# Turning a group's probabilities in two parts, and issuing the grams' rows from GpSimd

## The chip, the cores and the metric

The kernel runs on one core of a Trainium2 chip. Five engines of that core run their own streams of instructions and wait for each other by semaphores: TensorE (PE) multiplies matrices, VectorE (DVE), ScalarE (ACT) and GpSimd (POOL) work on elements, SyncE (SP) only issues DMA transfers. The metric is the device time of one execution in microseconds. The kernel before takes 424.8 us, the median of three runs (424.51 to 426.21).

## The reference

Cross attention with 20 heads of 16 channels over 8 batches: 112 queries, 375 context rows of 512 channels, of which the last four are image prompts.

```python
q = heads(hidden_states @ W_q)
k_t, v_t = heads(text_ehs @ W_k), heads(text_ehs @ W_v)
probs_t = softmax(einsum('bhsd,bhtd->bhst', q, k_t) * attn_scale)
text_out = einsum('bhst,bhtd->bhsd', probs_t, v_t)
attn_scores = einsum('bhsd,bhnd->bhsn', q, k_ip) * attn_scale
qsem = _l2norm(einsum('bhst,bte->bhse', probs_t, text_ehs))
sem = einsum('bhse,bne->bhsn', qsem, _l2norm(ip_ehs))
probs_ip = softmax(attn_scores + SEM_SCALE * sem) * spatial_mask[None, None, :, None]
out = (text_out + einsum('bhsn,bhnd->bhsd', probs_ip, v_ip)) @ W_out + b_out + hidden_states
```

All arithmetic is float32.

## The kernel before, in words

The norm of `qsem` is taken without forming `qsem`: it is p G p with G the gram matrix of the batch's context, so for every head the probabilities are multiplied once by a matrix `u` that holds the upper half of G (with doubled off-diagonal parts), the four prompts' products, a column of ones and the head's value columns.

The work goes in 40 steps `(b, g)`: 8 batches of 5 groups of 4 heads. In the main loop (35 steps) a step does this:

- `scores` (L709) multiplies one head's queries by its keys into a PSUM bank of a ring of two (`ps_sc`). `probabilities` (L738) takes the row maximum on VectorE (L742), the exponential on ScalarE (L745), and copies the prompts' four columns out (L747); `sent` (L751) has SyncE issue the transfer of the head's probabilities into `xg` (L754), one of two buffers, where they stand in blocks of 32 rows. This is done two steps ahead of the step that multiplies them: heads 2 and 3 at the head of the step (`now`), heads 0 and 1 during it (`then`). In the last steps of batch 6 `ahead` (L1238) draws some heads further forward; those in `more` are held, that is, sent later than computed.
- `transposed` (L756) turns the group of the next step: one VectorE transposition of all 12 blocks of `xg` into `xgT` (L762, 128 x 1536), for the last batch two of six blocks.
- `multiplied` (L768) is the main product: for each of 12 blocks j it issues four matmuls, one for each head, in four row groups of TensorE, into four PSUM banks (L781). Block j needs columns 32j to 392, so blocks get narrower: 392, 360, 328, ... 40. The right side is `u`; from batch 1 on, blocks 0 to 3 read its first third (c = 0), 4 to 7 the second, 8 to 11 the last. The function is a generator, and other work is issued between its blocks.
- After the product ScalarE copies the last 21 columns of each bank (`value_sums`, L794) and VectorE reduces the rest against the probabilities (`reduced`, L827, four instructions). Only then are the banks free for the next step, which uses the same four.
- `placed` (L681, L688) has GpSimd copy the next group's value columns into `u`, one copy for each third. The copy of a third must follow the blocks of this step that read that third, and precede those of the next step.
- `between` (L1116) gives TensorE the next batch's projections: the gram at g = 0 (`gram`, L516), values at g = 1, keys and values at 2, keys at 3, and the end of the batch before.

The next batch's gram is doubled by ScalarE into `ug` (L507), masked by GpSimd (L508, three instructions), and then carried by 16 transfers of 99 KB, `gram_to_groups` (L549, L553), into the other of two buffers `u`: four blocks of rows, each to four heads. In the kernel before, SyncE issues them in portions of two or four over steps g = 1 to 3, between the transfers of probabilities, context and values; batch 0's last block is issued by ScalarE.

The order of TensorE, SyncE, VectorE and ScalarE is that of the program text in the main loop. GpSimd's order there is made by a scheduler; only in the last batch it is that of the text too. A DMA waits on the issuing engine's stream for one of eight completion semaphores, so the ninth issue waits until the first transfer has landed.

Of the kernel before, what the change touches and what calls it, by code (L numbers as in the profile page):

```python
# [20 lines left out]
def kernel(  # L21
# [14 lines left out]
    nc = tc.nc  # L36
    P = 128
    B, S, C = x.shape
# [507 lines left out]
            doubled(ps[c][:, : T - c * P], c, half[:, c])  # L546
            yield

    def gram_to_groups(b, blocks, eng=nc.sync, parts=range(GROUP)):  # L549

        for q in blocks:
            for a in parts:
                eng.dma_start(  # L553
                    st[b]["u"][a * RG : (a + 1) * RG, q * GW : (q + 1) * GW],
                    ug[q * RG : (q + 1) * RG, :],
                )
# [152 lines left out]
    def scores(b, g, a, early=False, ps=None):  # L709
        s = st[b]  # L710
        _, qm, j = queries[b]
        i, r = g // 2, g % 2
        if early and (g + a // 2) % 2:

            ps = ps_qd.tile([P, 512], F32, tag="qd", name=f"ps_s_{b}_{g}_{a}")
        elif ps is None:
            ps = ps_sc.tile([P, 512], F32, tag="sc", name=f"ps_s_{b}_{g}_{a}")
        w = T if b > 0 else TT
        nc.tensor.matmul(  # L719
            ps[:S, :w],  # L720
            qm[a * RG : (a + 1) * RG, i, r, j * S : (j + 1) * S],
            s["kT"][a * RG : (a + 1) * RG, i, :w],
            start=True,
            stop=True,
        )
        s["sc", g, a] = ps
# [11 lines left out]
    def probabilities(b, g, a, hold=False):  # L738
        s = st[b]
        ps = s.pop(("sc", g, a))  # L740
        nmx = small.tile([S, 1], F32, tag="nmx", name=f"nmx_{b}_{g}_{a}", bufs=4)
        nc.vector.tensor_reduce(nmx, ps[:S, :TT], AX.X, ALU.max, negate=True)  # L742
        if ("p", g) not in s:
            s["p", g] = home(b, g)
        nc.scalar.activation(s["p", g][:, a, :], ps[:S, :TT], AF.Exp, bias=nmx)  # L745
        if b > 0:
            nc.scalar.copy(s["ipl"][:, groups[g][a], :], ps[:S, TT:T])  # L747
        if not hold:
            sent(b, g, a)

    def sent(b, g, a):  # L751

        xg = x_ring[(b * NG + g) % NX]
        nc.sync.dma_start(xg[a * RG : a * RG + S // QN, :, :TT], st[b]["p", g][:, a, :])  # L754

    def transposed(b, g):  # L756

        xg = x_ring[(b * NG + g) % NX]
        xT = work.tile([P, BLK, P], F32, tag="xgT", name=f"xgT_{b}_{g}")
        n = BLK // 2 if b == B - 1 else BLK  # L760
        for j in range(0, BLK, n):
            nc.vector.transpose(  # L762
                xT[:, j : j + n].rearrange("p j (k q) -> p q j k", q=QN),
                xg[:, :, j * RG : (j + n) * RG].rearrange("p q (j k) -> p q j k", k=RG),
            )
        st[b]["xT", g] = xT

    def multiplied(b, g):  # L768
        s = st[b]
# [406 lines left out]
    order_values()  # L1176
    drain(products)
    nc.scalar.preload_act_table(AF.Exp)
    gram_to_groups(0, range(QN - 1))
    run(("v", 0), lambda: values(0))  # L1180
    run(("q", 0), lambda: project_queries(pairs[0]), 3)
    gram_to_groups(0, (QN - 1,), nc.scalar)
# [22 lines left out]
    load_embed(nc.sync, wkip_sb, w_k_ip)  # L1205
    load_embed(nc.sync, wvip_sb, w_v_ip)
    placed(0, 0)
    transposed(0, 0)
    run(("k", 0), None)
    run(("v", 1), lambda: values(1))  # L1210
    more_constants()
# [38 lines left out]
    for n, (b, g) in enumerate(steps[:-NG]):  # L1250
        now, more, then = ahead(n)
        late = (b, g) == (0, NG - 2)
        for c, a in now if not late else ():
            scores(*c, a)
            probabilities(*c, a)
        for j, _ in enumerate(multiplied(b, g)):
            if j == 0:
                for c, a in now if late else ():
                    scores(*c, a)
                    probabilities(*c, a)  # L1260
                for c, a in more:
                    scores(*c, a, ps=bank(f"ps_s_{c[0]}_{c[1]}_{a}"))
                    probabilities(*c, a, hold=True)
            if j == 6:
                for c, a in then:
                    scores(*c, a)
            if j == 2:
                if g == 0:
                    gram_banks(b + 1)
                transposed(*steps[n + 1])  # L1270
                for c, a in more:
                    sent(*c, a)
                if 1 <= g <= 3:
                    gram_to_groups(b + 1, {1: (0,), 2: (1,), 3: (3,)}[g], parts=halves[g == 2])
                for c, i in x_loads.get((b, g), ())[: int(n > 0)]:
                    load_x_blocks(c, i)

                if g in (1, 2) and b > 0:
                    run(("f", b - 1), None)
        value_sums(b, g)  # L1280
        if g == 2 and b > 0:
            run(("f", b - 1), None)
        if n == NG - 1:
            run(("t", b), lambda: prompt_logits(b))
        for c, a in then:
            probabilities(*c, a)
        if n == len(steps) - NG - 1:
            sums = shared(b, g, GROUP // 2)
            next(sums)
            reduced(b, g, 2)  # L1290
        else:
            reduced(b, g)
        placed(*steps[n + 1])
        if g == 0 and b > 1:
            run(("f", b - 2), None)
        load_rest(n)
        if n == 0:
            load_next(2)
        if g in ctx_blocks and b < B - 3:
            load_ctx_blocks(b + 3, ctx_blocks[g])  # L1300
        for c, i in x_loads.get((b, g), ())[1:]:
            load_x_blocks(c, i)
        if g == 1:
            gram_to_groups(b + 1, (0,), parts=halves[1])
            gram_to_groups(b + 1, (1,), parts=halves[0])
        elif g == 2:
            gram_to_groups(b + 1, (2,))
        elif g == 3:
            gram_to_groups(b + 1, (3,), parts=halves[1])
            values_to_groups(b + 1)  # L1310
        if g in (2, 3) and b == 0:
            run(("pp",), None)
        if (b, g) == (B - 2, 0):
            prompt_values_by_head()
        if (b, g) == (B - 2, 1):
            bd = load_prompt_values_by_head()
        if (b, g) == (B - 2, 3):
            own_channels(bd)
        if g == 0 and b > 0:
            prompt_values(b - 1)  # L1320
        between(b, g)
        if g == 1:
            values_to_dram(b + 1, nc.sync, 0, 2)
        if g == 2:
            values_to_dram(b + 1, nc.sync, 2)
# [17 lines left out]
    for g in range(NG):  # L1343
        if g == 1:
            keys3 = last_keys(b, bank(f"ps_k_{b}_{FULL}", spare=True))
            next(keys3)
            next(keys3)
            run(("q", b), None)
            nc.scalar.preload_act_table(AF.Sqrt)
            run(before, None, 3)  # L1350
        for j, _ in enumerate(multiplied(b, g)):
            if g == 0 and j in (0, 3):
                for a in (2, 3) if j == 0 else (0, 1):
                    coming(NG - 2, a, bank(f"ps_s_{b}_{NG - 2}_{a}", spare=a > 1))
            if g == 0 and j in (2, 3):
                if j == 2:
                    transposed(b, 1)
                for a in (2, 3) if j == 2 else (0, 1):
                    sent(b, NG - 2, a)
            if g == 1 and j in (2, 3):  # L1360
                for a in ((3, 2), (1, 0))[j - 2]:
                    ps = ps_qd.tile([P, 512], F32, tag="qd", name=f"ps_s_{b}_{NG - 1}_{a}")
                    coming(NG - 1, a, ps)
            if g == 1 and j == 4:
                run(before, None)
            if g == 3 and j == 8:
                drain(sums)
            if 0 < g < NG - 1 and j in (QN - 1, 2 * QN - 1):
                placed(b, g + 1, (j // QN,))
        if g == NG - 1:  # L1370
            break
        n = (3, 3, 2, 1)[g]
        ahead, sums = sums, shared(b, g, n)
        next(sums)
        reduced(b, g, n)
        if g < NG - 2:
            value_sums(b, g, n)
            transposed(b, g + 2)
            placed(b, g + 1, range(NT) if g == 0 else (NT - 1,))
            next(sums)  # L1380
            drain(ahead)
        if g == 0:
            run(before, lambda: finish(b - 1, bd=bd[:, 0]))
            with_bias(b)
            run(("f", b - 2), None)
        if g == 2:
            nc.scalar.preload_act_table(AF.Sqrt)
        if g == 3:
            value_sums(b, g, 1, 3)
            placed(b, g + 1, (NT - 1,))  # L1390
            drain(sums)
            value_sums(b, g, 3)
            first = finish(b, (0, FULL * HC), bd=bd[:, 1])
            for _ in range(4):
                next(first)
# [70 lines left out]
```

## Time and profile before

| what | value |
|---|---|
| median of three runs | 424.8 us |
| profiled execution | 424.01 us, span 422.3 us |
| TensorE busy | 413.7 us (98%) |
| VectorE busy | 332.3 us (79%) |
| ScalarE busy | 185.2 us (44%) |
| GpSimd busy | 111.6 us (26%) |
| issues of `u<-ug` | 124 by SyncE, 4 by ScalarE |
| issues of `xg<-p` | 156 by SyncE |

Shares of busy time are over the whole span. Issuing a DMA is not counted as busy; it stands in the timeline with the engine's name and a q (SPq). The idle time of an engine stands in brackets behind the instruction that ended it, with what released it.

### The profile page before, as it was taken

What the parts mean: (1) busy time and instruction counts of PE and PEld (TensorE: products, weight loads), DVE (VectorE), ACT (ScalarE), POOL (GpSimd) and SP (SyncE); (2) the same over time, 40 slices, a digit from 0 to 9 for tenths busy, and PEclk for the clock granted to TensorE, in tenths of its full rate; (3) what the DMA queues carried; (4) which work ended last, traced back from release to release, by engine and by line L of the source; (5) the groups of instructions that cost most, each with busy time, mean ns of one, the idle gap of its engine ahead of it and who ended that gap; (6) DMA issues with size and microseconds to landing.
All of it is one profiled execution on the core that took longest, in us unless ns stands there. A gap on an engine that the chain in (4) does not pass through costs nothing.

```text
span 422.3 us, 14016 instructions
## 1 busy us (share of the span) xinstructions
PE 413.7 (98%) x5496; PEld 324.4 (77%) x5496; DVE 332.3 (79%) x693; ACT 185.2 (44%) x647; POOL 111.6 (26%) x277
## 2 busy tenths in 40 slices
PE   8999999999998999999999999999999999989996
PEld 8867768888776877788778877778778887778983
DVE  5036788879896978898789987887898987978774
ACT  2344332337333363344434363333634463445784
POOL 6411110012060111511142220602124222505540
PEclk9999999999999999999999999999999999999999
DMA  8676856666765555675656555655655456466200
GB/s 240 203 191 192 190 144 182 164 170 153 193 167 147 159 167 160 161 177 158 164 151 165 136 167 157 167 146 152 169 153 153 125 165 179 121 168 167 80 2 29
DMA packets 61687, 65.84 MB, mean 156 GB/s; under 512 B 22072, under 2 KB 55648, under 8 KB 61622
## 3 DMA queue, kind: packets, MB, share of 16 engines
q1 hardware_dynamic: 60990, 63.98, 56.6%
q8 instruction: 44, 0.72, 0.8%
q10 hardware_dynamic: 632, 0.96, 0.7%
q14 instruction: 21, 0.17, 0.1%
HBM read 20.23 MB, written 5.32 MB: 61 GB/s over the span
## 4 chain that ended last, share of the span: by engine, by line
PE 91%; DMA 2%; DVE 2%; issue 2%; ACT 2%; SPq 1%; POOL 0%; DVEq 0%; POOLq 0%
PE ps_qd L781 39%; PE ps_v L611 14%; PE ps_k L577 11%; PE ps_s L719 9%; PE ps_g L535 7%; PE ps_q L377 3%; PE ps_o L995 2%; PE ps_g L491 1%; DMA xg<-p 1%; DMA vipd<-ipkv 1%; DVE nmx L742 1%; PE ps_w L467 1%; PE ps_o L950 1%; PE ps_c L450 1%; DVE xgT L762 1%
## 5 line engine op out<-in xcount | busy, mean ns | idle before, releaser
L781 PE MATMUL ps_qd<-u,xgT 32*112 32x360 f32 (+11 forms) x3840 | 218.4, 351 | 2.0 <-POOL u L688 2.0
L781 PEld LDWEIGHTS ps_qd<-u,xgT 32*112 32x112 f32 x3840 | 187.3, 172 | 28.5 <-POOL u L688 3.1
L762 DVE STREAM_TRANSPOSE xgT<-xg 128x1536 f32<-128x1536 f32 (+1 forms) x45 | 119.7, 2677 | 11.4 <-DMA xg<-p 5.6
L745 ACT ACTIVATE p<-ps_s,nmx 112x371 f32<-112x371 f32 x156 | 85.2, 588 | 58.4 <-DVE nmx L742 46.5
L742 DVE TENSOR_REDUCE nmx<-ps_s 112x1 f32<-112x371 f32 x160 | 76.8, 524 | 28.2 <-PE ps_s L719 27.4
L827 DVE CUSTOM_DVE_ANT_0 junk<-ps_qd,p 112x371 f32<-112x371 f32 x146 | 79.1, 542 | 17.4 <-PE ps_qd L781 1.4
L688 POOL COPY u<-vr 128x64 f32<-128x64 f32 x120 | 26.0, 239 | 152.4 <-PE ps_qd L781 91.8
L719 PE MATMUL ps_s<-kT,qm 32*112 32x375 f32 (+1 forms) x320 | 65.7, 496 | 0.0
L611 PE MATMUL ps_v<-wv_sb,ctxT 128*128 128x384 f32 (+1 forms) x192 | 63.0, 477 | 0.0
L611 PEld LDWEIGHTS ps_v<-wv_sb,ctxT 128*128 128x128 f32 x192 | 35.7, 190 | 20.9
L794 ACT COPY pvs<-ps_qd 112x21 f32<-112x21 f32 x151 | 16.3, 189 | 75.1 <-PE ps_qd L781 72.3
L577 PE MATMUL ps_k<-ctxT,wk_sb 128*128 128x371 f32 x136 | 46.9, 488 | 0.2 <-DVE ctxT L458 0.2
L577 PEld LDWEIGHTS ps_k<-ctxT,wk_sb 128*128 128x128 f32 x136 | 24.4, 189 | 14.0 <-issue 0.5
L719 PEld LDWEIGHTS ps_s<-kT,qm 32*112 32x112 f32 x320 | 23.3, 170 | 12.3 <-issue 10.8
L535 PE MATMUL ps_g<-ctxT 128*32 128x375 f32 (+11 forms) x672 | 30.4, 333 | 0.0
L535 PEld LDWEIGHTS ps_g<-ctxT 128*32 128x32 f32 x672 | 27.7, 110 | 2.0
L618 ACT COPY vext<-ps_v 128x384 f32<-128x384 f32 (+1 forms) x24 | 11.2, 466 | 39.5 <-PE ps_v L611 39.0
L747 ACT COPY ipl<-ps_s 112x4 f32<-112x4 f32 x140 | 24.5, 175 | 0.0
L386 DVE TENSOR_SCALAR qm<-ps_q,emask 128x224 f32<-128x224 f32 (+1 forms) x25 | 9.0, 395 | 18.3 <-PE ps_q L377 18.2
L970 POOL TENSOR_TENSOR wv<-vip,w 112x1280 f32<-112x1280 f32 x6 | 14.8, 2466 | 26.2 <-DVE w L910 26.2
L437 DVE STREAM_TRANSPOSE ctxT<-ct 128x512 f32<-128x512 f32 x18 | 19.9, 1107 | 0.0
L508 POOL TENSOR_TENSOR ug<-ug,half 128x128 f32<-128x128 f32 (+1 forms) x24 | 10.5, 449 | 30.9 <-ACT ug L507 30.9
(174 smaller groups left out, 319.3 us busy)
## 6 DMA issues: line engine op xcount, KB each, us to landing
xg<-p SPq DMA_DIRECT2D x156, 162.3 KB
u<-ug SPq DMA_DIRECT2D x124, 99.0 KB
ct<-in_ctx_dram SPq DMA_DIRECT2D x24, 176.0 KB
vr<-vd SPq DMA_DIRECT2D x32, 120.0 KB
vip<-vipd SPq DMA_DIRECT2D x6, 560.0 KB
vd<-vext SPq DMA_DIRECT2D x7, 320.0 KB
vd<-vext SPq DMA_DIRECT2D x7, 160.0 KB
out_dram<-ob SPq DMA_DIRECT2D x8, 140.0 KB
```

The lines of the kernel that those rows point to most:

```text
L437: nc.vector.transpose(ctxT[:, :, c * P : (c + 1) * P].rearrange("p e (j i) -> p j e i", i=RG), ct[:, some, :].rearrange("p j (k e) -> p j ...
L535: nc.tensor.matmul(ps[c][q * RG : (q + 1) * RG, j * RG - c * P : T - c * P], ctxT[:, e, j * RG : (j + 1) * RG], ctxT[:, e, j * RG : T], st ...
L577: nc.tensor.matmul(ps[:, :TT], wk_sb[:, e, i * P : (i + 1) * P], s["ctxT"][:, e, :TT], start=(e == 0), stop=(e == NE - 1),)
L611: nc.tensor.matmul(ps[:, :w], ctxT[:, e, c * P : (c + 1) * P], wv_sb[:, e, :w], start=(e == 0), stop=(e == NE - 1),)
L688: nc.gpsimd.tensor_copy(v, dealt(b, c, s["vr"][:, c * QN : (c + 1) * QN, g, :]))
L719: nc.tensor.matmul(ps[:S, :w], qm[a * RG : (a + 1) * RG, i, r, j * S : (j + 1) * S], s["kT"][a * RG : (a + 1) * RG, i, :w], start=True, st ...
L742: nc.vector.tensor_reduce(nmx, ps[:S, :TT], AX.X, ALU.max, negate=True)
L745: nc.scalar.activation(s["p", g][:, a, :], ps[:S, :TT], AF.Exp, bias=nmx)
L747: nc.scalar.copy(s["ipl"][:, groups[g][a], :], ps[:S, TT:T])
L762: nc.vector.transpose(xT[:, j : j + n].rearrange("p j (k q) -> p q j k", q=QN), xg[:, :, j * RG : (j + n) * RG].rearrange("p q (j k) -> p ...
L781: nc.tensor.matmul(banks[a][:S, j * RG : UW], xT[a * RG : (a + 1) * RG, j, :S], region(b, c)[a * RG : (a + 1) * RG, q, j * RG - c * P :], ...
L827: nc.vector.tensor_tensor_reduce(out=junk, in0=ps[:S, :TT], in1=s["p", g][:, a, :], scale=1.0, scalar=0.0, op0=ALU.mult, op1=ALU.add, accu ...
```

## The change

Two things change. The turn of a group in the main loop becomes a generator: eight blocks are turned at j = 2, then, at j = 5 instead of 6, the scores of heads 0 and 1 are issued, followed at once by their maxima and exponentials (they stood after `value_sums` before), and then the other four blocks are turned. Heads whose buffer is the one just turned are sent after that. The last batch's own turns keep their two halves. The main loop so has 34 more transpositions, and each is 1024 or 512 wide instead of 1536.

And `gram_to_groups` issues from GpSimd unless told otherwise; only three blocks of batch 0 stay with SyncE and one with ScalarE. That moves 112 issues, 16 for each of seven batches.

```diff
-    def gram_to_groups(b, blocks, eng=nc.sync, parts=range(GROUP)):
+    def gram_to_groups(b, blocks, eng=nc.gpsimd, parts=range(GROUP)):
...
-    def transposed(b, g):
+    def turned(b, g, n=BLK // 2):
         xg = x_ring[(b * NG + g) % NX]
         xT = work.tile([P, BLK, P], F32, tag="xgT", name=f"xgT_{b}_{g}")
-        n = BLK // 2 if b == B - 1 else BLK
-        for j in range(0, BLK, n):
+        st[b]["xT", g] = xT
+        for j0 in range(0, BLK, n):
+            j1 = min(j0 + n, BLK)
             nc.vector.transpose(
...
-        st[b]["xT", g] = xT
+            yield
...
-    gram_to_groups(0, range(QN - 1))
+    gram_to_groups(0, range(QN - 1), nc.sync)
...
-            if j == 6:
+            if j == 5:
                 for c, a in then:
                     scores(*c, a)
+                held = more + [(c, a) for c, a in then if c == steps[n + LEAD + 1]]
+                for c, a in then:
+                    probabilities(*c, a, hold=(c, a) in held)
+                drain(turn)
+                for c, a in held:
+                    sent(*c, a)
             if j == 2:
                 if g == 0:
                     gram_banks(b + 1)
-                transposed(*steps[n + 1])
-                for c, a in more:
-                    sent(*c, a)
+                turn = turned(*steps[n + 1], 2 * QN)
+                next(turn)
...
-        for c, a in then:
-            probabilities(*c, a)
```

In the built program GpSimd's stream for one batch (here the part after batch 3's masks of the next gram; the batches 1 to 6 are alike) stands in this order, L553 being the moved issues, L877 the division that stood at L876, and L688 one third of `placed`:

```
L508 TensorTensor ug<-ug,half x3
L553 DMACopy u<-ug 32x792 x3
L877 TensorTensor attn<-pvs,zr 112x320
L553 DMACopy u<-ug 32x792 x5
L688 TensorCopy u<-vr 128x4x16
L553 DMACopy u<-ug 32x792 x6
L688 TensorCopy u<-vr 128x4x16
L553 DMACopy u<-ug 32x792 x2
L688 TensorCopy u<-vr 128x4x16
```

The three L688 there are `placed(b, 2)`, thirds 0, 1 and 2. In the kernel before the same stream is L508 x3, L876, L688 x3. In batch 0 the order after the masks is 11 issues, third 0 of `placed(0, 2)`, 5 issues, thirds 1 and 2.

More of the change, by code (lines that the diff above doesn't have):

```diff
@@ L754, in sent @@
         nc.sync.dma_start(xg[a * RG : a * RG + S // QN, :, :TT], st[b]["p", g][:, a, :])
-    def transposed(b, g):
+    def turned(b, g, n=BLK // 2):
         xg = x_ring[(b * NG + g) % NX]
         xT = work.tile([P, BLK, P], F32, tag="xgT", name=f"xgT_{b}_{g}")
-        n = BLK // 2 if b == B - 1 else BLK
-        for j in range(0, BLK, n):
+        st[b]["xT", g] = xT
+        for j0 in range(0, BLK, n):
+            j1 = min(j0 + n, BLK)
             nc.vector.transpose(
-                xT[:, j : j + n].rearrange("p j (k q) -> p q j k", q=QN),
-                xg[:, :, j * RG : (j + n) * RG].rearrange("p q (j k) -> p q j k", k=RG),
+                xT[:, j0:j1].rearrange("p j (k q) -> p q j k", q=QN),
+                xg[:, :, j0 * RG : j1 * RG].rearrange("p q (j k) -> p q j k", k=RG),
             )
-        st[b]["xT", g] = xT
+            yield
     def multiplied(b, g):
@@ L1207 @@
     placed(0, 0)
-    transposed(0, 0)
+    drain(turned(0, 0, BLK))
     run(("k", 0), None)
@@ L1356 @@
                 if j == 2:
-                    transposed(b, 1)
+                    drain(turned(b, 1))
                 for a in (2, 3) if j == 2 else (0, 1):
@@ L1377 @@
             value_sums(b, g, n)
-            transposed(b, g + 2)
+            drain(turned(b, g + 2))
             placed(b, g + 1, range(NT) if g == 0 else (NT - 1,))
```

## The prediction

> **What bounds the kernel now.** I read the page's busy times and chain first, then the busy times by stretch, then TensorE's timeline for its pauses.
>
> ```profile
> span 422.3 us, 14016 instructions
> PE 413.7 (98%) x5496; PEld 324.4 (77%) x5496; DVE 332.3 (79%) x693; ACT 185.2 (44%) x647; POOL 111.6 (26%) x277
> ...
> PE 91%; DMA 2%; DVE 2%; issue 2%; ACT 2%; SPq 1%; POOL 0%; DVEq 0%; POOLq 0%
> ```
>
> ```profile
> 280.00:340.00 60.00, 60.00 (x879) 48.06 (x875) 51.34 (x109) 26.27 (x100) 14.31 (x34) 1.00 0.54 146
> 340.00:400.00 60.00, 58.58 (x819) 47.38 (x815) 49.26 (x99) 32.73 (x116) 23.55 (x40) 1.00 0.55 152
> ```
>
> ```profile
> 87.65 3.89 PE L781 MATMUL ps_qd<-u,xgT 32*112 32x392 f32 x54 [0.62 <-POOL u L688]
> ...
> 135.91 0.54 PE L568 MATMUL ps_k<-ident,k 128*128 128x128 f32 x3 [1.32 <-ACT ipl L747]
> ...
> 379.99 1.29 PE L781 MATMUL ps_qd<-u,xgT 32*112 32x392 f32 x10 [1.36 <-POOL u L688]
> ```
>
> TensorE is the bound: from 280 to 340 us it is busy 60.00 us of 60, in the next stretch, with the last pause, 58.58, both at a granted clock of 1.00 (the columns are length, then busy time of PE, PEld, DVE, ACT and POOL, then clock). Where it never pauses nothing can be gained; only its three pauses above, 0.62 + 1.32 + 1.36 = 3.30 us, can go. But anything that comes late for a product is paid in full.
>
> **What the change takes away.** The pauses go back to SyncE.
>
> ```profile
> 80.32 1.23 SPq L553 DMA_DIRECT2D u<-ug  x2
> 81.60 2.17 SPq L636 DMA_DIRECT2D vr<-vd  x4
> 87.36 0.59 POOL L688 COPY u<-vr 128x64 f32<-128x64 f32 x3 [6.55 <-DMA vipd<-ipkv]
> ...
> 128.75 2.02 SPq L553 DMA_DIRECT2D u<-ug  x2
> 131.90 2.97 DVE L762 STREAM_TRANSPOSE xgT<-xg 128x1536 f32<-128x1536 f32 x1 [2.62 <-issue]
> ...
> 372.90 2.14 SPq L553 DMA_DIRECT2D u<-ug  x2
> 375.09 2.15 SPq L636 DMA_DIRECT2D vr<-vd  x4
> 379.70 0.59 POOL L688 COPY u<-vr 128x64 f32<-128x64 f32 x3 [10.89 <-DMA xg<-p]
> ```
>
> ```profile
> L553 SPq DMA_DIRECT2D u<-ug x124: 575/589/2139, 14.9 to 374.3; - x124
> ```
>
> The first and the last pause are value rows that land late, issued behind gram rows; in the second a group turned 2.62 us late made the exponentials late that free a bank. Without 112 issues of 0.589 us, 16 for a batch, SyncE reaches each of these transfers at least two issues (1.2 us) sooner, and the probabilities of heads 0 and 1 are sent sooner too, since their exponentials no longer stand behind `value_sums`. I take all of 3.30 us as gone; left is what is late next, at worst none of it goes.
>
> **The turn in two parts.** VectorE's price is the fixed part of one more transposition.
>
> ```profile
> L762 DVE STREAM_TRANSPOSE xgT<-xg 128x1536 f32<-128x1536 f32 x35 | 104.6, 2989 | 11.4 <-DMA xg<-p 5.6 <-issue 3.0 <-DMA ct<-in_ctx_dram 2.6
> ...
> L437 DVE STREAM_TRANSPOSE ctxT<-ct 128x512 f32<-128x512 f32 x18 | 19.9, 1107 | 0.0
> ```
>
> From 512 to 1536 columns is 1882 ns, 1.84 ns each; so 1024 cost 2.05 us, and the two parts 3.16 us against 2.99, 0.17 us more in each of 34 steps. It matters where VectorE is last at the banks:
>
> ```profile
> 225.98 0.54 DVE L827 CUSTOM_DVE_ANT_0 junk<-ps_qd,p 112x371 f32<-112x371 f32 x1
> 226.47 3.41 PE L781 MATMUL ps_qd<-u,xgT 32*112 32x392 f32 x48
> ```
>
> There, from group 3 to 4, the fourth bank is free at 226.52 and wanted at 226.47: no slack. VectorE runs without a break from the step before, so up to two of these 0.17 us show, 0.3 us in each of six batches: 0 to 2.1 us. If TensorE pauses in a batch for something longer (next part), VectorE catches up meanwhile and the price is nothing; I take that. The maxima only change places with the last third of the turn, and nothing waits longer for either: the next step's product wants `xgT` only after `between`. If a maximum had to wait for its scores, the turn behind it would wait too, at most the 0.5 us of one maximum. ScalarE's copies of the sums now stand behind two exponentials. They hold the banks as `reduced` does, but are shorter:
>
> ```profile
> L827 DVE CUSTOM_DVE_ANT_0 junk<-ps_qd,p 112x371 f32<-112x371 f32 x146 | 79.1, 542 | 17.4 <-PE ps_qd L781 1.4
> ...
> L794 ACT COPY pvs<-ps_qd 112x21 f32<-112x21 f32 x151 | 16.3, 189 | 75.1 <-PE ps_qd L781 72.3
> ```
>
> Four are 0.8 us against 2.2 for VectorE's, so they stay hidden unless the exponentials end over 1.4 us after the product. In the last two steps of batch 6 the held heads are sent at j = 5 instead of 2, some 2 us later; their group is turned a step later, so I cost it at nothing, and at 2 us each if that cover is gone.
>
> **The gram's rows on GpSimd.** This decides. Each batch moves 16 issues into a stream that also carries `placed`, and 14 of them stand ahead of its second third (3 before the division, 5 and 6 around third 0). No row shows an issue by GpSimd. Batch 3 before:
>
> ```profile
> 197.00 0.84 POOL L508 TENSOR_TENSOR ug<-ug,half 128x128 f32<-128x128 f32 x2 [1.10 <-ACT ug L507]
> 201.28 0.74 POOL L876 TENSOR_TENSOR attn<-pvs,zr 112x320 f32<-112x320 f32 x1 [3.44 <-DVE zr L888]
> ...
> 210.41 0.24 POOL L688 COPY u<-vr 128x64 f32<-128x64 f32 x1 [7.86 <-PE ps_qd L781]
> ```
>
> ```profile
> 207.08 0.58 PE L781 MATMUL ps_qd<-u,xgT 32*112 32x392 f32 x2
> ...
> 212.43 2.76 PE L577 MATMUL ps_k<-ctxT,wk_sb 128*128 128x371 f32 x8
> ```
>
> The masks end at 197.84. Step (3, 2) runs 207.08 to 212.43, about 4.95 us without its scores; blocks 0 to 3 are 1376 of 2592 columns, so block 4 starts at 207.08 + 2.63 = 209.71 (the copy at 210.41, which is released when block 3 is through, lies 0.7 us behind it). Until then GpSimd has 11.87 us for 14 issues of d, the division and two copies, 0.74 + 0.48 = 1.22 us. The wait is 14d + 1.22 - 11.87 us. Third 2 then comes after 2d + 0.24, wanted 864 columns and the scores later, 1.65 + 0.4 = 2.05 us.
>
> How long is d? Its ends: 0.12 us, GpSimd's smallest instruction, and 1.52 us, SyncE's longer issue scaled as below.
>
> ```profile
> L204 POOL MEMSET half<- 32x32 f32 x12 | 1.4, 117 | 0.5
> ```
>
> ```profile
> L754 SPq DMA_DIRECT2D xg<-p x156: 800/859/1559, 26.8 to 397.4; - x156
> ```
>
> ```profile
> L961 DVE TENSOR_TENSOR ob<-ps_o,xb 112x320 f32<-112x320 f32 x7 | 3.4, 485 | 0.3 <-PE ps_o L995 0.3
> ```
>
> ```profile
> L841 POOL TENSOR_TENSOR xb<-x_sb,bias_sb 112x320 f32<-112x320 f32 x7 | 6.1, 867 | 29.1 <-DMA x_sb<-in_x_dram 17.8 <-PE ps_s L719 11.3
> ```
>
> The nearest row is SyncE's 0.589 us for the very same transfer. But the same addition takes GpSimd 867 ns and VectorE 485, 1.79 times as long, and I expect GpSimd to be the slower at issuing too. Scaled whole, 0.589 becomes 1.05 us; some part of an issue is handing over that should cost alike on both, so I take 1.0 us, an estimate. The Trainium skill, DMA: Bandwidth & Descriptors, Specifications, puts the first byte at about 1 us on GpSimd's path and about 0.6 us on SP's. An estimate from these two figures is 0.98 us for an issue, by which the waits below would sum to about 22 us; no run shows it yet.
>
> With 1.0 the wait at third 1 is 14 + 1.22 - 11.87 = 3.35 us, at third 2 another 2.24 - 2.05 = 0.19: 3.54 us in each of batches 2 to 5, 14.2 us. Batches 0, 1 and 6 have other rooms:
>
> ```profile
> 47.14 0.84 POOL L508 TENSOR_TENSOR ug<-ug,half 128x128 f32<-128x128 f32 x2 [0.66 <-ACT ug L507]
> ...
> 98.01 0.84 POOL L508 TENSOR_TENSOR ug<-ug,half 128x128 f32<-128x128 f32 x2 [0.90 <-ACT ug L507]
> 103.41 0.74 POOL L876 TENSOR_TENSOR attn<-pvs,zr 112x320 f32<-112x320 f32 x1 [4.55 <-DVE zr L888]
> ...
> 341.73 0.84 POOL L508 TENSOR_TENSOR ug<-ug,half 128x128 f32<-128x128 f32 x2 [1.11 <-ACT ug L507]
> ```
>
> ```profile
> 59.69 0.58 PE L781 MATMUL ps_qd<-u,xgT 32*112 32x392 f32 x2
> 108.40 0.58 PE L781 MATMUL ps_qd<-u,xgT 32*112 32x392 f32 x2
> ...
> 350.95 0.58 PE L781 MATMUL ps_qd<-u,xgT 32*112 32x392 f32 x2
> ```
>
> Batch 1: 98.85 to 108.40 + 2.63, 12.18 us. Its division started at 103.41 and comes 0.94 us sooner with the shorter turn, 3.62 us after the masks where three issues take 3.0, so 0.6 is lost: 3.6 + 0.2 = 3.8 us. Batch 6: 11.01 us of room, 4.2 + 0.2 = 4.4 us. Batch 0 has 16 issues and two copies, 16.48 us, in 47.98 to 62.32: 2.1 us. Sum 14.2 + 3.8 + 4.4 + 2.1 = 24.5 us, all of it TensorE's pause. The ninth issue waits for the first transfer to land; value rows landed some 3.6 us after their issue (83.77 to 87.36), eight issues take 8 us, so that costs nothing. If landing took over 8 us it would add the difference once a batch.
>
> **Sum.** 24.5 for GpSimd's issues, 0 for VectorE, -3.3 for SyncE: 21.2 us more. The profiled execution took 424.0 us (its span and 1.7 around it), so 445.2; the median of the runs stands 0.8 above it, which gives 446.
>
> **Rivals.** *GpSimd issues as fast as SyncE*: the other side. The division's input comes 2.5 us after the masks, and 2.5 + 0.74 + 0.48 + 11d fits into 11.87 as long as d is below 0.74. Then no product waits, and at 0.589 the sum is -3.3 plus 0 to 2.1 for VectorE, 421.5 to 423.6 on the median's scale, say 422.5. For it: the transfer is the same, and GpSimd waits far more than it works:
>
> ```profile
> L688 POOL COPY u<-vr 128x64 f32<-128x64 f32 x120 | 26.0, 239 | 152.4 <-PE ps_qd L781 91.8
> ```
>
> Against it: the 1.79 of the addition, and that those 91.8 us are waits for products, which the new order fills with issues ahead of the copy that is wanted. The same page of the Trainium skill, in its section on the anatomy of one DMA, calls the dispatch some 50 ns and descriptor generation small and variable; by that rule this rival holds.
>
> *Between*: d of 0.74 to 0.8. At 0.8 the waits are 0.65 us in batches 2 to 5 (0.1 of it for the division) and about 1.4 and 1.5 in batches 1 and 6, 5.5 us, less 3.3: 427; at 0.77 425. The two halves of the change cancel.
>
> *Much slower*: each 0.1 us of d is 1.6 us a batch in seven batches, 11 us. At 1.2 that makes 468, at 1.52 504. Or the pauses cost clock: the longest of the three above, 1.36 us, left it at 1.00 in its stretch, so a longer one is untried. If each of the seven let blocks 4 to 11 run at half speed, 4.95 - 2.63 = 2.3 us more, that is 16 us, 462. The Trainium skill, TensorE: Matmul & The Clock Gate, in its section on HAM oscillation, wants no pause above some 3.4 us, and by that rule mine of 3.35 us stand at the edge.
>
> **Chances.** 0.57 for d of 0.8 to 1.2 (427 to 468), 0.13 for more than 1.2 or lost clock, 0.23 for fast issues, 0.07 for between. About 0.5%, 2.1 us, is what a measurement can tell from no change, so 422.7 divides the fast case: 0.18 below, 0.05 inside, since its 422.5 lies at the limit and the pauses may give a little more than the three that I count. Between gives 0.05 inside, 0.02 slower. Faster 0.18, same 0.10, slower 0.72. A range for 8 times in 10 must reach the fast case at one end and d = 1.2 at the other, 421 to 468; the likeliest case alone spans 427 to 468.
>
> **What would show it.** Issues of about 1 us on GpSimd's queue at L553; in steps (b, 2) a pause of TensorE between blocks 3 and 4, released by POOL u, some 3.4 us long, and one for batch 0; TensorE's busy share down from 98% to 93%; POOL in the chain. The three old pauses gone, SyncE's waits shorter, transpositions of 2.05 and 1.11 us. I am wrong if GpSimd's issues come closer than 0.74 us: then no pause at (b, 2), and what is left is the 3.3 us and VectorE's 0.17 us a step.

## The result, and the profile after

The changed kernel takes 428.97 us, the median of six runs (427.95 to 433.17); the kernel before, run beside it, 425.07. The ratio is 1.0123, with a 95% interval of 1.0083 to 1.0164: slower, by about a fifth of what was predicted. Ratios, here and in the table of the experiments, go by the fast runs alone, so they need not be the quotients of the medians beside them. The profiled execution took 427.95 us with a span of 426.1, 3.8 more than before.

The page of the changed kernel: its span, its busy times and the chain of work that ended last.

```profile
span 426.1 us, 14059 instructions
PE 418.1 (98%) x5496; PEld 326.5 (77%) x5496; DVE 336.4 (79%) x727; ACT 182.8 (43%) x647; POOL 167.3 (39%) x389
...
q1 hardware_dynamic: 55614, 52.62, 46.6%
q0 software_dynamic: 3584, 11.36, 11.9%
...
PE 86%; DMA 6%; DVE 5%; ACT 1%; issue 1%; DVEq 0%; SPq 0%; ACTq 0%
```

POOL is not in the chain at all. Its busy time has grown from 111.6 to 167.3 us because an issue by GpSimd, unlike one by SyncE, is counted as busy. What has come into the chain is DMA, 6% where it was 2%. The queue lines show packets, MB and share of the 16 DMA engines: the grams' 11.36 MB now go by a queue of their own, q0, beside SyncE's q1. TensorE is busy 98% as before and still ends later, so the loss does not show as idle time: a product that waits between its matmuls counts as busy.

The groups and waits of the changed kernel that answer to the issues and turns shown of before (busy time, mean ns, then idle time before them):

```profile
L553 POOL DMA_DIRECT2D u<-ug x112 | 55.7, 502 | 10.7 <-DMA u<-ug 7.9 <-POOL ug L508 2.1 <-issue 0.6
...
L688 POOL COPY u<-vr 128x64 f32<-128x64 f32 x120 | 27.0, 240 | 96.0 <-PE ps_qd L782 58.9 <-DMA vr<-vd 36.3 <-PE ps_kip L321 0.6
```

```profile
DVE xgT L763 <- DMA xg<-p: 11.0, 7, 3.2
...
PEld ps_qd L782 <- DVE ss L828: 1.5, 4, 0.4
```

An issue takes GpSimd 0.50 us, not 1.0, and its value copies wait for the product, not the product for them: no wait of TensorE names GpSimd's copies into `u` any more. VectorE, however, waits 11.0 us for sends of probabilities, in seven places, up to 3.2 us; before it was 5.6 us in all. Here are these turns in VectorE's timeline (start, length, the idle time before in brackets):

```profile
64.79 2.03 DVE L763 STREAM_TRANSPOSE xgT<-xg 128x1024 f32<-128x1024 f32 x1 [3.21 <-DMA xg<-p]
113.33 2.03 DVE L763 STREAM_TRANSPOSE xgT<-xg 128x1024 f32<-128x1024 f32 x1 [1.83 <-DMA xg<-p]
162.55 2.05 DVE L763 STREAM_TRANSPOSE xgT<-xg 128x1024 f32<-128x1024 f32 x1 [1.45 <-DMA xg<-p]
259.36 2.03 DVE L763 STREAM_TRANSPOSE xgT<-xg 128x1024 f32<-128x1024 f32 x1 [0.17 <-DMA xg<-p]
308.77 2.04 DVE L763 STREAM_TRANSPOSE xgT<-xg 128x1024 f32<-128x1024 f32 x1 [0.48 <-DMA xg<-p]
357.89 2.05 DVE L763 STREAM_TRANSPOSE xgT<-xg 128x1024 f32<-128x1024 f32 x1 [2.45 <-DMA xg<-p]
```

Six of the seven are in a step (b, 2); the other, 1.43 us in (0, 0), was there before. Step (b, 2) turns what step (b, 1) sends, and (b, 1) is where GpSimd now issues most of a batch's 16 rows, one behind the other. The chain of the changed kernel shows how long those sends take (issue, then time to landing), and the chain of the kernel before what one took when it was last there:

```profile
57.54 7.13 DMA xg<-p
...
105.86 7.36 DMA xg<-p
113.33 2.03 DVE xgT L763
...
123.84 0.57 ACT p L745
124.51 0.96 PE ps_s L719 x3
...
350.64 7.13 DMA xg<-p
```

```profile
126.87 2.97 DMA xg<-p
```

7.1 to 7.4 us against 3.0. The one shown of before stands at another step. The same sends can be followed in both traces by their packets, 112 of 1484 bytes each. The last send of a step (b, 1) is issued 7.0 to 8.3 us into the step after, 7.4 to 9.4 before; its last packet ends 5.0 to 6.7 us after the issue, where it was 2.4 to 3.8. So each is issued 0.4 to 1.5 us sooner and still arrives 1.5 to 3.3 us later. The reason is in the stretches around the second of the three sends shown (last columns: granted clock, share of the 16 DMA engines, GB/s; packets are counted by their start, so a share can pass 1), first after, then before:

```profile
103.00:107.00 4.00, 4.00 (x57) 2.89 (x50) 3.14 (x7) 2.79 (x10) 4.00 (x9) 1.00 1.03 259
107.00:111.00 4.00, 4.00 (x29) 2.19 (x31) 2.61 (x7) 0.96 (x2) 2.59 (x7) 1.00 0.99 229
111.00:115.00 4.00, 4.00 (x93) 3.73 (x85) 2.17 (x3) 1.15 (x4) 1.63 (x6) 1.00 1.11 251
```

```profile
103.00:107.00 4.00, 4.00 (x16) 2.39 (x13) 3.57 (x13) 2.90 (x10) 1.27 (x4) 1.00 0.83 178
107.00:111.00 4.00, 4.00 (x41) 2.57 (x43) 2.52 (x4) 1.59 (x5) 0.00 (x0) 1.00 0.81 222
111.00:115.00 4.00, 4.00 (x78) 3.49 (x71) 3.86 (x8) 0.82 (x7) 0.91 (x4) 1.00 0.67 184
```

The DMA engines are full for twelve microseconds, where they had room. In the kernel before, the gram's rows stood between the sends in SyncE's one queue; now they move beside them.

How a late turn reaches TensorE, in VectorE's and TensorE's timelines of the same step and the next:

```profile
116.46 0.99 DVE L742 TENSOR_REDUCE nmx<-ps_s 112x1 f32<-112x371 f32 x2
117.36 1.10 DVE L763 STREAM_TRANSPOSE xgT<-xg 128x512 f32<-128x512 f32 x1
...
120.39 0.54 DVE L828 CUSTOM_DVE_ANT_0 junk<-ps_qd,p 112x371 f32<-112x371 f32 x1
```

```profile
120.24 0.58 PE L782 MATMUL ps_qd<-u,xgT 32*112 32x392 f32 x2
120.64 0.48 PE L719 MATMUL ps_s<-kT,qm 32*112 32x375 f32 x2
120.66 3.73 PE L782 MATMUL ps_qd<-u,xgT 32*112 32x392 f32 x46
```

The maxima and the reductions stand behind the turn, so the fourth bank is free only at 120.93, while step (1, 3) has wanted it since 120.66; that row lasts 3.73 us where the same stretch of the product took 3.41 before:

```profile
119.45 3.41 PE L781 MATMUL ps_qd<-u,xgT 32*112 32x392 f32 x48
```

Most of what this step loses comes after it: by the chain above, the scores at 124.51 wait for a bank that an exponential of 123.84 frees, and that one stands behind the next maxima of the late VectorE.

Set against the kernel before, step by step (from the first matmul of each step in TensorE's two timelines), the loss and the waits for sends stand together:

| batch | VectorE's wait for sends in (b, 2) | lost by steps (b, 2) and (b, 3) |
|---|---|---|
| 0 | 3.21 | 2.50 |
| 1 | 1.83 | 1.63 |
| 2 | 1.45 | 0.74 |
| 3 | 0 | 0.29 |
| 4 | 0.17 | 0 |
| 5 | 0.48 | 0.39 |
| 6 | 2.45 | 2.46 |

That is 8.0 us lost. (In batch 3 the same turn stood idle for 0.39 us, but the profile puts that down to no transfer.) The three steps (0, 4), (1, 4) and (6, 4), in which the old pauses lay, give back 1.15, 1.53 and 1.44, 4.1 us; all else is -0.1, which makes the 3.8 us of the span.

### The profile page after: what moved, and what is told of

Same layout as the page of the kernel before. It is cut to its first block, busy times and chain, and to the rows that moved or that the text cites. A ratio compares the mean times of both kernels' runs of the same rounds, so it can differ in the third digit from the quotient of the medians.

```text
span 426.1 us, 14059 instructions
## 1 busy us (share of the span) xinstructions
PE 418.1 (98%) x5496; PEld 326.5 (77%) x5496; DVE 336.4 (79%) x727; ACT 182.8 (43%) x647; POOL 167.3 (39%) x389
## 3 DMA queue, kind: packets, MB, share of 16 engines
q0 software_dynamic: 3584, 11.36, 11.9%
## 4 chain that ended last, share of the span: by engine, by line
PE 86%; DMA 6%; DVE 5%; ACT 1%; issue 1%; DVEq 0%; SPq 0%; ACTq 0%
PE ps_qd L782 38%; PE ps_v L611 11%; PE ps_s L719 10%; PE ps_k L577 9%; PE ps_g L535 7%; DMA xg<-p 5%; PE ps_q L377 3%; PE ps_o L996 3%; DVE xgT L763 1%; PE ps_g L491 1%; DVE nmx L742 1%; DMA ip_sb<-in_ctx_dram 1%; ACT p L745 1%; PE ps_o L951 1%; PE ps_k L593 1%
## 5 line engine op out<-in xcount | busy, mean ns | idle before, releaser
L782 PE MATMUL ps_qd<-u,xgT 32*112 32x168 f32 (+11 forms) x3840 | 223.7, 352 | 0.0
L782 PEld LDWEIGHTS ps_qd<-u,xgT 32*112 32x112 f32 x3840 | 189.6, 172 | 27.2 <-DVE ss L828 1.5
L745 ACT ACTIVATE p<-ps_s,nmx 112x371 f32<-112x371 f32 x156 | 84.3, 578 | 125.6 <-DVE nmx L742 118.5
L763 DVE STREAM_TRANSPOSE xgT<-xg 128x512 f32<-128x512 f32 (+2 forms) x79 | 125.8, 1601 | 11.7 <-DMA xg<-p 11.0
L742 DVE TENSOR_REDUCE nmx<-ps_s 112x1 f32<-112x371 f32 x160 | 78.1, 532 | 25.5 <-PE ps_s L719 24.7
L719 PE MATMUL ps_s<-kT,qm 32*112 32x375 f32 (+1 forms) x320 | 68.6, 499 | 0.9 <-ACT kT L584 0.8
L688 POOL COPY u<-vr 128x64 f32<-128x64 f32 x120 | 27.0, 240 | 96.0 <-PE ps_qd L782 58.9
L553 POOL DMA_DIRECT2D u<-ug x112 | 55.7, 502 | 10.7 <-DMA u<-ug 7.9
L719 PEld LDWEIGHTS ps_s<-kT,qm 32*112 32x112 f32 x320 | 27.0, 171 | 14.7 <-issue 10.7
L577 PEld LDWEIGHTS ps_k<-ctxT,wk_sb 128*128 128x128 f32 x136 | 24.5, 190 | 14.0 <-issue 0.5
L747 ACT COPY ipl<-ps_s 112x4 f32<-112x4 f32 x140 | 23.0, 164 | 0.0
L508 POOL TENSOR_TENSOR ug<-ug,half 128x128 f32<-128x128 f32 (+1 forms) x24 | 10.4, 446 | 30.9 <-ACT ug L507 30.9
```

The lines of the kernel that those rows point to most:

```text
L553: eng.dma_start(st[b]["u"][a * RG : (a + 1) * RG, q * GW : (q + 1) * GW], ug[q * RG : (q + 1) * RG, :],)
L577: nc.tensor.matmul(ps[:, :TT], wk_sb[:, e, i * P : (i + 1) * P], s["ctxT"][:, e, :TT], start=(e == 0), stop=(e == NE - 1),)
L688: nc.gpsimd.tensor_copy(v, dealt(b, c, s["vr"][:, c * QN : (c + 1) * QN, g, :]))
L719: nc.tensor.matmul(ps[:S, :w], qm[a * RG : (a + 1) * RG, i, r, j * S : (j + 1) * S], s["kT"][a * RG : (a + 1) * RG, i, :w], start=True, st ...
L763: nc.vector.transpose(xT[:, j0:j1].rearrange("p j (k q) -> p q j k", q=QN), xg[:, :, j0 * RG : j1 * RG].rearrange("p q (j k) -> p q j k", ...
L782: nc.tensor.matmul(banks[a][:S, j * RG : UW], xT[a * RG : (a + 1) * RG, j, :S], region(b, c)[a * RG : (a + 1) * RG, q, j * RG - c * P :], ...
```

## The experiments

Theory A: the gram's rows on a second queue take the DMA engines from the sends, and the turns wait. Theory B: VectorE's and ScalarE's new order costs. Theory C: GpSimd's issues cost, by holding up its copies. The runs were taken in three sets (e1 to e4, e5 to e8, e9 to e12), and each set has its own runs of the kernel before (median 424.85, 424.35 and 426.23 us), so ratios are compared rather than times:

| run | rows a batch on GpSimd | time, us | ratio to before, 95% interval |
|---|---|---|---|
| the changed kernel | 16 | 428.97 | 1.0123 (1.0083 to 1.0164) |
| e1, turn only | 0 | 421.59 | 0.9973 (0.9932 to 1.0013) |
| e2, rows only | 16 | 432.33 | 1.0176 (1.0118 to 1.0234) |
| e3, half of the rows | 8 | 422.53 | 0.9964 (0.9933 to 0.9996) |
| e4, rows apart | 16 | 426.83 | 1.0053 (1.0024 to 1.0081) |
| e5, 16 extra rows | 16 extra | 433.03 | 1.0246 (1.0189 to 1.0303) |
| e6, 16 tiny extra | 16 tiny | 423.15 | 0.9992 (0.9960 to 1.0024) |
| e7, rows apart, copy early | 16 | 422.47 | 0.9966 (0.9939 to 0.9993) |
| e8, half, old turn | 8 | 422.79 | 0.9983 (0.9949 to 1.0017) |
| e9, three quarters | 12 | 426.68 | 1.0053 (1.0016 to 1.0089) |
| e10, half and apart | 8 | 420.89 | 0.9881 (0.9846 to 0.9915) |

**The two parts alone (e1, e2).**

```diff
# e1, on the changed kernel
-    def gram_to_groups(b, blocks, eng=nc.gpsimd, parts=range(GROUP)):
+    def gram_to_groups(b, blocks, eng=nc.sync, parts=range(GROUP)):
# e2, on the kernel before
-    def gram_to_groups(b, blocks, eng=nc.sync, parts=range(GROUP)):
+    def gram_to_groups(b, blocks, eng=nc.gpsimd, parts=range(GROUP)):
-    gram_to_groups(0, range(QN - 1))
+    gram_to_groups(0, range(QN - 1), nc.sync)
```

> The turn in two parts alone; every gram's row is on SyncE's queue again. Theory A (the gram's rows on GpSimd's queue run beside the probabilities' sends and make them land some 7 us after their issue, so that VectorE's turn in step (b, 2) waits): no turn waits over 0.5 us for a send in the steps (b, 2), and the time is within 0.5% of the kernel before, 423 to 427 us. Theory B (the new order on VectorE and ScalarE, maxima between the parts and exponentials ahead of the copies of the sums, frees the banks late): the loss of the whole change is here, 428 to 430 us. Theory C (GpSimd's issues hold up its own copies of values): as A.

> The gram's rows on GpSimd alone, with the turn in one piece and the order of the kernel before. Theory A: the turns of the steps (b, 2) wait for their sends, some 11 us in all as in the changed kernel, and the time is 428 to 430 us. Theory B: the pauses that came from SyncE are gone and nothing takes their place, 421 to 423 us. Theory C: GpSimd's copies of values come late and TensorE waits for POOL u; time above that of the kernel before.

The turn alone is not to be told from no change; the rows alone cost 1.76%. The wait and two links of the chain of e2:

```profile
DVE xgT L762 <- DMA xg<-p: 17.2, 11, 3.8
```

```profile
253.84 8.24 DMA xg<-p
...
353.90 8.16 DMA xg<-p
```

Theory B falls, and A holds so far, with two misses of size: in e1 one turn in a step (b, 2) waited 0.96 us, and e2 lost more than the whole change, with sends of up to 8.2 us. In one place of e2, step (6, 2), TensorE also pauses before block 4 for GpSimd's copy, as theory C has it:

```profile
360.69 1.44 PE L781 MATMUL ps_qd<-u,xgT 32*112 32x264 f32 x24 [1.01 <-POOL u L688]
```

GpSimd's issues ahead of that copy wait 2.3 us in all for earlier rows to land. Whether the new turn softens the loss (1.76% without it, 1.23% with it) stays open, since the intervals overlap.

**Bytes or issues (e5, e6).** The kernel before with 16 more transfers a batch from GpSimd, into DRAM that nobody reads, so they change no result. In e5 GpSimd's stream has them at the places where the changed kernel has its rows. In e6 the scheduler placed them otherwise: 4 behind the first mask, 7 behind the others and 5 behind the division, so all 16 stand ahead of the copies into `u`.

```diff
                     ug[q * RG : (q + 1) * RG, :],
                 )
+                if b > 0:   # e6: 8 in place of GW
+                    nc.gpsimd.dma_start(st[b]["extra"][q, a, :, :GW], ug[q * RG : (q + 1) * RG, :GW])
```

> The kernel before, its gram's rows on SyncE as they were, and beside them GpSimd issues a batch's 16 rows once more, the same 101 KB each, into memory that nobody reads; GpSimd's stream is then that of the changed kernel, issue for issue. Theory A (the bytes beside the sends cost): sends of step (b, 1) land 7 us or later after their issue, turns wait over 11 us in all, and the time is at least 1% above the kernel before, 430 us or more. Theory C (the issues in GpSimd's stream cost): the same loss, but with the wait at POOL.

> As the run beside it, the same 16 issues a batch at the same places of GpSimd's stream, but of 8 columns in place of 792, 1 KB each. Theory A: no bytes, no loss, within 0.5% of the kernel before, 423 to 427 us. Theory C: the loss of the run beside it stays, 430 us.

The issues last the same in both, in the lines of e5 and then of e6:

```profile
L559 POOL DMA_DIRECT2D extra<-ug x112 | 55.6, 502 | 9.9 <-DMA extra<-ug 7.2 <-POOL ug L509 2.1 <-issue 0.4
```

```profile
L559 POOL DMA_DIRECT2D extra<-ug x112 | 55.8, 504 | 5.0 <-DMA extra<-ug 2.9 <-POOL ug L509 2.1
```

With 101 KB each they cost 2.5%, with 1 KB nothing that can be measured. So theory C falls as the cause of the loss: the price is in the bytes, not in GpSimd's time. In one place of e6 the issues do hold up the copies, here a link of its chain and a row of TensorE's timeline:

```profile
339.18 6.41 DMA extra<-ug
```

```profile
350.39 3.76 PE L784 MATMUL ps_qd<-u,xgT 32*112 32x392 f32 x56 [0.83 <-POOL u L691]
```

The second transfer of the 16 issued in step (6, 1) lands only after 6.4 us, the tenth issue waits for it, the copies stand behind the issues, and the step lasts 1.7 us longer than before. The steps of the old pauses, (0, 4), (1, 4) and (6, 4), give back 0.8, 1.3 and 1.4 us in the same trace, although every row of the gram is still with SyncE. What e5 waits for is mixed (9.5 us of VectorE's waits are put down to sends, 5.5 to context, 5.3 to gram's rows), since the grams are still on SyncE and the bytes come on top; that it would be sends alone was too narrow.

**Less at once (e3, e9, e8).** Every second row on SyncE; in e9 every fourth; e8 is e3 on the kernel before with its turn in one piece.

```diff
-                eng.dma_start(
+                (nc.sync if b > 0 and a % 2 else eng).dma_start(   # e9: a == GROUP - 1
```

> The changed kernel with every second row of the gram on SyncE's queue, eight issues a batch on each engine. Theory A: half as many bytes stand beside the sends, they land 2 to 3 us sooner, the turns wait under half of the 11.0 us, and the time is 425 to 427 us. Theory B: as the changed kernel, 429 us. Theory C: GpSimd has half of the issues, time about that of the kernel before; A and C are told apart by which wait has gone, DVE xgT for the sends or POOL.

> The changed kernel with every fourth row of the gram on SyncE: 12 issues a batch on GpSimd, between the 8 of the run with half of them (0.36% faster) and the 16 of the changed kernel (1.23% slower). Theory A: the loss begins where the rows no longer fit beside the sends, so it lies between the two, 423 to 428 us, and VectorE waits for the sends in some of the steps (b, 2). If GpSimd's issues cost each for itself, it is on the line between the two, 426 us.

> Every second row of the gram on GpSimd, with the turn in one piece and the order of the kernel before. If the turn in two parts is worth its 0.3% only where nothing competes with the sends, this is 422 to 424 us, the same as with the new turn; if the earlier sends of the new turn are what makes half of the rows harmless, it is 425 to 428 us.

0, 8, 12 and 16 rows give 0.9973, 0.9964, 1.0053 and 1.0123: flat up to half, then up. An equal price for every row would have shown between 0 and 8; e9 by itself fits both theories, and its VectorE waits 10.4 us for sends. That half of the rows cost nothing was a miss: 425 to 427 us were expected of e3. In e3 VectorE waits for a send only once:

```profile
41.66 2.12 DVE L763 STREAM_TRANSPOSE xgT<-xg 128x1024 f32<-128x1024 f32 x1 [2.63 <-DMA xg<-p]
```

That is in step (0, 0), where no gram's row is on the way. From (2, 0) to (5, 3) every step of e3 starts 2.3 to 2.4 us before the same step of the kernel before, so each takes what it took there and the further transposition costs nothing; in (6, 2) and (6, 3) 1.7 us are lost still, where the turn waits 1.77 us for a transfer of values (`vd<-vext`). e8 shows no loss either, so it is not the new turn that makes half of the rows harmless.

**The same bytes, apart (e4, e7).** In e4 GpSimd's stream follows the program, which puts 2 to 6 rows between the copies of three steps; e7 also moves the prompts' copy into `ctxT` forward to j = 2 of step (b, 0).

```diff
-    ctx.enter_context(tc.manual_schedule(engines=engines | {mybir.EngineType.Activation}))
+    ctx.enter_context(tc.manual_schedule(
+        engines=engines | {mybir.EngineType.Activation, mybir.EngineType.Pool}))
# e7, the copy of L520 from gram(b) to gram_banks(b)
+        nc.gpsimd.tensor_copy(st[b]["ctxT"][:, :, TT:T], ipnT[:, :, b * NIP : (b + 1) * NIP])
...
-        nc.gpsimd.tensor_copy(ctxT[:, :, TT:T], ipnT[:, :, b * NIP : (b + 1) * NIP])
```

> The changed kernel with GpSimd's stream in the order of the program, so that a batch's 16 rows no longer stand together behind the masks but two to six at a time between the copies of values of three steps. The same issues and bytes. Theory A: fewer of them run beside the second pair's sends of step (b, 1), the waits of the turns for sends fall to under half of 11.0 us, and the time is 424 to 427 us. Theory B: 429 us. Theory C: the issues still stand between the same copies, 428 to 430 us.

> The paced kernel lost 0.65 to 0.76 us at the start of each of seven grams, where TensorE waited for GpSimd's copy into ctxT, which the order of the program puts behind the six copies of values; here that copy stands two blocks into the step before it. Theory A: those seven waits are gone, 4.8 us, and with the rows apart nothing else is lost: 421 to 423 us, the same as with half of the rows on SyncE. If the rows beside the sends still cost, it stays at 425 to 427 us.

e4 still loses, but its waits name another place, GpSimd's copy that the gram needs; VectorE's wait for sends is 5.8 us, about half:

```profile
PE ps_g L535 <- POOL ctxT L520: 4.8, 7, 0.8
```

With that copy early these seven waits are gone and all 112 rows on GpSimd are 0.34% faster than before. VectorE still waits 7.2 us for sends in e7, 2.6 of them in (0, 0), where no row is on the way; the waits of (0, 2) and (6, 2), 2.3 and 1.4 us, cost 1.5 and 0.2. In the steps (1, 1) to (6, 1), whose sends were late, GpSimd issues 8 rows in e4 and e7, as many as in e3, where the changed kernel has 11 to 15. So GpSimd's queue as such costs nothing; the loss goes with how many of its rows run beside the sends of that step.

**Both cures (e10)**, e3's edit on e7.

> Half of the rows on SyncE and the other half on GpSimd in the order of the program, with the copy into ctxT early: the two cures together. If anything of the competition is left in either, this is the fastest of all, 420 to 422 us; if both had taken it away whole, it is the same as each, 422 to 423 us.

```profile
PE 98%; DVE 1%; POOL 0%; issue 0%; POOLq 0%; DVEq 0%
```

The chain is TensorE alone for 98%, and the time is 420.89 us, 0.85 to 1.54% under the kernel before in its set and 1.6 us under e3 and e7 by the medians of different sets. The kernel before had its highest median in that set, so the ratio may flatter. Step by step, e3 still loses 1.7 us in (6, 2) and (6, 3) and e7 1.5 in (0, 3); e10 loses 0.5 in (0, 3) and 0.2 in (5, 3). GpSimd issues 4 rows in each of the steps (1, 1) to (6, 1) there. It beats both kernels.

**The two kernels once more (e11, e12).**

> The kernel before once more, for its three pauses of 0.62, 1.32 and 1.36 us. If they come from SyncE's queue alone they are all there again at the same steps; if one of them hangs on how the transfers of one execution fall, it is missing or of another length.

> The changed kernel once more, for the waits of the turns. Theory A: VectorE waits for sends in most of the steps (b, 2) again, 8 to 14 us in all, with the largest losses in the first and the last batches, where other loads are on the way as well.

```profile
89.35 1.11 PE L781 MATMUL ps_qd<-u,xgT 32*112 32x392 f32 x7 [0.58 <-POOL u L688]
...
138.24 0.54 PE L568 MATMUL ps_k<-ident,k 128*128 128x128 f32 x3 [1.55 <-ACT ipl L747]
...
381.56 1.28 PE L781 MATMUL ps_qd<-u,xgT 32*112 32x392 f32 x10 [0.62 <-POOL u L688]
```

The three pauses are there again, 0.58, 1.55 and 0.62 us; their places hold, their sizes do not, which by the expectation means that at least one hangs on how the transfers of one execution fall. The changed kernel repeats too: 13.5 us of waits for sends, and sends of 6.0 and 7.9 us in its chain at the first and the last batch.

## Why the prediction was wrong

**The price of an issue (the step that failed).** "How long is d?" took 1.0 us, scaling SyncE's 0.589 by the 1.79 that an addition costs GpSimd. It is 0.50 us in 112 of them, less than SyncE's. By the prediction's own bound, no wait below 0.74, the 24.5 us become nothing, and so they did: no pause between blocks 3 and 4 in a step (b, 2). The nearest row was the same transfer on SyncE, without the scaling; how fast an engine adds said nothing of how fast it issues. The Trainium skill's first byte of about 1 us (DMA: Bandwidth & Descriptors, Specifications), from which 0.98 was estimated, is a time to arrival and not what the engine is held for; the measured 0.50 decides against that estimate. Its section on the anatomy of one DMA, with a small dispatch and generation, was the better guide.

**The missing term (the second step that failed).** The sum moved 112 issues and gave their bytes no price. That SyncE is relieved and "the probabilities of heads 0 and 1 are sent sooner too" was booked as a gain. They are sent sooner, the last of a step (b, 1) by 0.4 to 1.5 us, and arrive 1.5 to 3.3 us later, because rows that used to stand between them in one queue now share the DMA engines with them: 8.0 us. e5 and e6 show that it is the bytes. So the rival with fast issues, 422.5 us, had the right d and the wrong time, and the forecast had the right sign for a wrong reason. A rule against the change stood in the Trainium skill, in the section Issuing engines are not separate DMA queues of the same page: transfers run on the same 16 DMA engines and interleave whoever issues them, and a second issuer only saves issue time. The runs agree with it, and it was not weighed.

**What held, and what of it stays open.** The three pauses went, and their steps give 4.1 us for the 3.30 taken; e3 and e10 are 2.0 and 3.4 us ahead where the last batch begins. That SyncE's 16 issues made the pauses is not shown. e6 leaves all of them with SyncE and its trace has none of the three; e1 does too and has lost the second whole and 0.8 us of the third. So the size was right, and the reason is open. The turn in two parts costs nothing that can be measured (e1, and the steps of e3). The parts last 2.03 and 1.10 us in the rows shown, against 2.05 and 1.11 worked out.

**What was right only in its outcome.** The ninth issue's wait was put at nothing because a landing takes 3.6 us and eight issues 8. Eight take 4.0, the landing 4.9 us in the median and 7.1 at most, and GpSimd waits 7.9 us in eight places; in this kernel no product waits for what stands behind it there. It was near: in e2 one did, for 1.0 us in step (6, 2), and e6 lost 1.7 us in step (6, 1) that way. And TensorE's busy share did not fall, although it lost 8 us: these waits are inside products.

## What to carry to other kernels

Moving a transfer to another engine's queue takes away its place behind the transfers that matter: ask what it will now run beside, and look at the share of the DMA engines in that stretch before asking what an issue costs. If the stretch is near full, leave part of the transfers where they are, or put other work of the issuing engine between them; half on each queue, in the order of the program, came out 1.2% under the kernel before here. When a bound engine ends later without more idle time, compare the start of each step in two timelines and look at what its rows last.

## What the runs showed of the hardware

An issue of the 32 x 792 row holds GpSimd for 0.496 us in the median and SyncE for 0.589. With 8 columns in place of 792 it holds GpSimd as long (0.504 against 0.502 us in the mean). By the packets in the traces, a row goes from GpSimd's queue in 16 packets of 6336 bytes, two of its 32 lines each, and from SyncE's in 32 packets of 3168; 16 packets of 4 bytes come with it on either (3584 packets for 112 rows against 5376). A send of 162 KB lands in 3.0 to 3.2 us in four rows of the chains of the kernel before, and in 6.0 to 8.2 us beside these rows. The Trainium skill (DMA: Bandwidth & Descriptors, Queues, rings and completion order) has a DMA engine alternate between queues packet by packet, by which larger packets would take the larger share; the longer landings agree with sharing, and no run here varied the size of the rows' packets by itself.
